# A graph network's second layer: edge directions computed chunk by chunk inside the loop, and eighteen buffers for the summed messages in place of eight

## The chip, the core and the metric

The kernel runs on one core of a Trainium2 chip. The core has a matrix engine (TensorE, PE in the profile; its weight loads are PEld), VectorE (DVE), ScalarE (ACT), GpSimd (POOL) and SyncE (SP). SP and POOL also issue DMAs here: SP plain loads and stores, POOL the indirect gathers and scatters. The metric is device time in microseconds, from launch to end; lower is better. A profiled execution gives for every instruction its start, its duration and what released it.

## The reference: what is computed

Two message-passing layers over a graph of 12500 nodes and 212500 edges (100000 pairs in both directions and 12500 loops, sorted by `dst`). A node has 160 features: 64 scalars and 32 vectors of three components. The change touches the second layer only. Cut to what matters there:

```python
h = relu(layernorm(x))
s, v = h[:, :64] @ W_nl0, einsum('nmi,mk->nki', h[:, 64:].reshape(N, 32, 3), W_nl1)
rhat = edge_attr / norm(edge_attr)                # (E, 3): the direction of an edge
w0..w4 = split(relu(edge_feature @ W_fc1) @ W_fc2)
xs, xv = s[dst], v[dst]
tp = concat(w0*xs, w3*(xv . rhat), (w1*xs) x sh1, w2*xv, w4*cross(xv, sh1)/sqrt2)   # sh1 = sqrt3 * rhat
agg = segment_sum(tp, src) / 32
```

For every edge the kernel thus needs its direction (three components over their length), the weights from its 64 edge features, and the row of its `dst` node; it forms 480 products per edge and adds them to the row of the `src` node.

## The kernel before

Edges are handled in tiles of 128 (one edge per partition): T = 1668 tiles. G = 4 tiles make a **quad** (417 of them, the passes `q` of the second layer's loop), CT = 12 tiles make a **chunk** (139, index `ch`), so a chunk is three quads. The work goes in stages: node maps, the first layer's loop over the edges, a short stage in between, the second layer's loop, and the output stage. All of the change lies in the second layer's loop and in the short stage right before it.

*Before the loop* (lines 684 to 692). A tile `r` of shape [128, 3, 1668] float32 (20016 bytes in every partition) is kept for the whole loop. Twelve passes each load 139 tiles' worth of edge vectors (`ea`, two buffers), and `directions` (line 613) makes the unit vectors: DVE squares (L615) and sums over the three components (L617), ACT takes the root (L618), DVE the reciprocal (L619) and the product (L620). These instructions are left to the scheduler's order.

*Loads of a chunk* (`sources`, `loads`, lines 699 to 715, all on SP): the `src` numbers of the chunk (`rows`, L702), the edge features (`ft`, L708), and four times the `dst` numbers of 384 edges (`to`, L713) and a window of 32 node rows (`fw`, L714). `picks` (L717) lets DVE compare `to` with the window's node numbers, which gives the 0/1 matrix `pick`.

*A quad in the loop* (lines 795 to 814) goes through these steps; the numbers tell for which quad a pass `q` does them:

- `hide(q + 4)`: PE multiplies the edge features (`hp`, L730), ACT takes the relu (`hs`, L732).
- `weights(q + 2, ...)`: PE makes the weights `wp` (L740; PSUM, two buffers).
- `picked(q + 3, ...)`: PE picks the `dst` rows (`gs`, L757) and ACT spreads them into `xs` and `xv` (L630 to L633).
- `turns(q + 2)`: ACT copies the quad's directions out of `r` (L624, L626) and the `src` numbers (L766) into spare columns of `wp`.
- `alike` (L665): DVE compares the quad's `src` numbers with each other (`same`); `second_messages` (L638): DVE makes the 480 products per edge (`msg`), eight instructions.
- `scattered(q, j)` for each of the four tiles: PE adds up equal `src` (`sm`, L771, two PSUM buffers), ACT copies the sum to `o` (L773, eight buffers), POOL issues the indirect DMA that adds `o` to the rows of accumulator `acc1[t % K]` in HBM (L775). K is 4, so tile t and tile t - 4 add to the same accumulator.

What sets the order: nearly every instruction in this loop goes through `keep`, which pins it on its engine behind everything that was traced on this engine before it. So PE, ACT and DVE run the loop in the order in which it is written:

```python
if (q + 4) % (CT // G) == 0:
    picks((q + 4) // (CT // G))
same = alike(...)
msg = second_messages(...)
scattered(q, 0, same, msg)
weights(q + 2, 0)
scattered(q, 1, same, msg)
picked(q + 3, 0)
weights(q + 2, 1)
scattered(q, 2, same, msg)
picked(q + 3, 1)
turns(q + 2)
scattered(q, 3, same, msg)
hide(q + 4)
```

Ahead of the loop stand `sources(0)`, `loads(0)`, `loads(1)`, `picks(0)`, `picks(1)` and the first `hide`, `weights`, `turns` and `picked`.

Of the kernel before, what the change touches and what calls it, by code (L numbers as in the profile page):

```python
# [9 lines left out]
F32 = mybir.dt.float32  # L10
# [3 lines left out]
AF = mybir.ActivationFunctionType  # L14
ALU = mybir.AluOpType
AX = mybir.AxisListType
# [3 lines left out]
P = 128  # L20
# [8 lines left out]
T = 1668  # L29
EP = T * P  # L30
PAD = N + 12
S = 3
# [8 lines left out]
G = 4  # L41
NQ1 = T // G
CT = 12
# [7 lines left out]
C1 = 480  # L51
# [5 lines left out]
def gnn_kernel(ctx: ExitStack, tc: tile.TileContext, a, out):  # L57
    nc = tc.nc
    tt = nc.vector.tensor_tensor
# [85 lines left out]
    for m in range(3):  # L145
        f0 = m * 96
        while f0 < (m + 1) * 96:
            k, p0 = divmod(f0, P)
            n = min((m + 1) * 96 - f0, P - p0)
# [127 lines left out]
    ep = edges0.enter_context(tc.tile_pool(name="ep0", bufs=1))  # L277
# [50 lines left out]
    def keep(i):  # L328
        tc.keep_in_program_order(i)
# [138 lines left out]
    with edges0 as st:  # L468
        ld = st.enter_context(tc.tile_pool(name="ld0", bufs=2))
        gp = st.enter_context(tc.tile_pool(name="gp0", bufs=6))  # L470
        wk = st.enter_context(tc.tile_pool(name="wk0", bufs=4))
# [49 lines left out]
        for gr in range(NG):  # L521
            hidden["now"] = gr
            q, a_ = divmod(gr, 2)
# [50 lines left out]
    with tc.tile_pool(name="okw", bufs=1) as wk, tc.tile_pool(name="okp", bufs=1, space=PSUM) as ps:  # L574
# [24 lines left out]
        m = NCB - 1  # L599
# [10 lines left out]
        nc.vector.tensor_copy(ok, over)  # L610


    def directions(su, r, ea, n):
        sq = su.tile([P, n, 3], F32, name="sq3")
        tt(sq, ea, ea, ALU.mult)  # L615
        no = su.tile([P, n], F32, name="no")
        nc.vector.tensor_reduce(no, sq, AX.X, ALU.add)  # L617
        nc.scalar.activation(no, no, AF.Sqrt)  # L618
        nc.vector.reciprocal(no, no)  # L619
        tt(r.rearrange("p m t -> p t m"), ea, no[:, :, None].to_broadcast([P, n, 3]), ALU.mult)  # L620

    def turned(r7, r, n, keep=lambda i: i):

        keep(nc.scalar.copy(r7[:, 0:6].rearrange("p (k m) t -> p k m t", m=3),  # L624
                            r[:, None, :, :].to_broadcast([P, 2, 3, n])))
        keep(nc.scalar.copy(r7[:, 6:7], r[:, 0:1]))  # L626
# [55 lines left out]


    with ExitStack() as st:
        ep = st.enter_context(tc.tile_pool(name="ep1", bufs=1))
        r = ep.tile([P, 3, T], F32, name="r")
        with tc.tile_pool(name="su1", bufs=2) as su:
            n = T // 12
            for i in range(12):
                ea = su.tile([P, n, 3], F32, name="ea")  # L690
                nc.sync.dma_start(ea, a["ea3"][:, i * n * 3:(i + 1) * n * 3])
                directions(su, r[:, :, i * n:(i + 1) * n], ea, n)
        ld = st.enter_context(tc.tile_pool(name="ld1", bufs=2))
        gp = st.enter_context(tc.tile_pool(name="gp1", bufs=3))
        wk = st.enter_context(tc.tile_pool(name="wk1", bufs=2))
        ps = st.enter_context(tc.tile_pool(name="ps1", bufs=1, space=PSUM))
        part = {}

        def sources(ch):
            if ch < NCH:  # L700
                part["rows", ch] = ld.tile([P, CE], I16, name="rows")
                nc.sync.dma_start(part["rows", ch], a["src_low"][:, ch * CE:(ch + 1) * CE].to_broadcast([P, CE]))  # L702

        def loads(ch):
            if ch >= NCH:
                return
            ft = ld.tile([P, CT // 2 * P], F32, name="ft")
            nc.sync.dma_start(ft, a["ea64"][:, ch * (CT // 2 * P):(ch + 1) * (CT // 2 * P)])  # L708
            to = ld.tile([P, S * P], I16, name="to")
            fw = ld.tile([P, D], F32, name="fw", bufs=3)  # L710
            for k in range(CW):
                e = ch * CE + k * S * P
                nc.sync.dma_start(to[k * W:(k + 1) * W, :], a["dst_low"][:, e:e + S * P].to_broadcast([W, S * P]))  # L713
                hidden["write"] = nc.sync.dma_start(fw[k * W:(k + 1) * W, :], ft1[bass.ds(row(ch * CW + k, NP - W), W), :])  # L714
            part["ft", ch], part["to", ch], part["fw", ch] = ft, to, fw

        def picks(ch):  # L717

            if ch < NCH:
                pick = ld.tile([P, S, P], F32, name="pick")  # L720
                keep(nc.vector.tensor_scalar(pick.rearrange("p t e -> p (t e)"), part["to", ch], nf[:, ch:ch + 1],
                                             None, op0=ALU.is_equal))
                part["pick", ch] = pick

        def hide(q):
            if q >= NQ1:
                return
            ch, k = divmod(q, CT // G)
            hp = ps.tile([P, 2 * P], F32, name="hp")
            keep(nc.tensor.matmul(hp, w1_1, part["ft", ch][:, k * 2 * P:(k + 1) * 2 * P], start=True, stop=True))  # L730
            part["hs", q] = wk.tile([P, 2 * P], F32, name="hs", bufs=3)
            keep(nc.scalar.activation(part["hs", q], hp, AF.Relu))  # L732

        def weights(q, c):
            if q >= NQ1:
                return
            if c == 0:
                part["wp", q] = ps.tile([P, G, 256], F32, name="wp", bufs=2)
            for h in range(2):
                keep(nc.tensor.matmul(part["wp", q][:, 2 * h + c, :224],  # L740
                                      part["hs", q][h * 64:(h + 1) * 64, c * P:(c + 1) * P],
                                      w1_2[h * 64:(h + 1) * 64], start=True, stop=True))

        def picked(q, i):
            if q >= NQ1:
                return
            ch, k = divmod(q, CT // G)
            if i == 0:
                part["xs", q] = gp.tile([P, G, S0], F32, name="xs")
                part["xv", q] = gp.tile([P, GV, G, V1], F32, name="xv")  # L750

            cut = S - k * G % S
            lo, hi = (cut, G) if i else (0, cut)
            gs = ps.tile([P, S, D], F32, name="gs")
            for j in range(lo, hi):
                u, v = divmod(k * G + j, S)
                keep(nc.tensor.matmul(gs[:, j - lo, :], part["pick", ch][u * W:(u + 1) * W, v, :],  # L757
                                      part["fw", ch][u * W:(u + 1) * W, :], start=True, stop=True))
            spread(part["xs", q][:, lo:hi], part["xv", q][:, :, lo:hi], gs[:, 0:hi - lo], keep)

        def turns(q):

            if q < NQ1:
                few = part["wp", q][:, 0, 224:256].rearrange("p (c t) -> p c t", t=G)
                turned(few[:, 0:7], r[:, :, q * G:(q + 1) * G], G, keep)
                keep(nc.scalar.copy(few[:, 7], idx["src"][:, q * G:(q + 1) * G]))  # L766
                part["few", q] = few

        def scattered(q, j, same, msg):
            sm = ps.tile([P, C1], F32, name="sm", bufs=2)  # L770
            keep(nc.tensor.matmul(sm, same[:, j, :], msg[:, j, S0:], start=True, stop=True))  # L771
            o = wk.tile([P, C1], F32, name="o", bufs=8)
            keep(nc.scalar.copy(o, sm))  # L773
            t = q * G + j
            nc.gpsimd.indirect_dma_start(  # L775
                out=acc1[t % K][:, :], out_offset=bass.IndirectOffsetOnAxis(ap=where[:, t:t + 1], axis=0),
                in_=o, in_offset=None, compute_op=ALU.add)

        sources(0)
        loads(0)
        loads(1)
        picks(0)
        picks(1)
        for q in range(4):
            hide(q)
        for q in range(3):
            if q < 2:
                weights(q, 0)  # L790
                weights(q, 1)
                turns(q)
            picked(q, 0)
            picked(q, 1)
        for q in range(NQ1):
            ch, k = divmod(q, CT // G)
            t0 = q * G
            if k == 0:
                sources(ch + 1)
                loads(ch + 2)  # L800
            if (q + 4) % (CT // G) == 0:
                picks((q + 4) // (CT // G))
            same = alike(wk, part["rows", ch][:, k * G * P:(k + 1) * G * P], part["few", q][:, 7], G, keep)
            msg = second_messages(wk, part["wp", q], part["xs", q], part["xv", q], part["few", q][:, 0:7], G, keep)
# [10 lines that stand above are left out]
# [14 lines left out]
    with tc.tile_pool(name="fwk", bufs=4) as wk, tc.tile_pool(name="fps", bufs=3, space=PSUM) as ps:  # L829
# [18 lines left out]
        for i in range(len(parts) + 1):  # L848
            now, ready = ready, added(i + 1)
            if now:  # L850
                t, s = now
# [3 lines left out]
            if gated:  # L855
                c, lo, n = parts[i - 1]
# [40 lines left out]
    with tc.If(flag > 0):  # L897
        with tc.tile_pool(name="gwk", bufs=1) as wk, tc.tile_pool(name="gps", bufs=1, space=PSUM) as ps:
# [14 lines left out]
            with tc.For_i(0, NQ) as q:  # L913
# [4 lines left out]
                for a_ in range(2):  # L918
# [4 lines left out]
                    for j in range(S):  # L923
                        t = HALF[a_][j]
# [43 lines left out]
            with tc.For_i(0, T // G) as q:  # L968
# [10 lines left out]
                for j in range(G):  # L979
                    h, c = divmod(j, 2)  # L980
# [67 lines left out]
```

## Time and profile before

| | |
|---|---|
| median of 13 runs | 6351.79 us (6329.0 to 6366.49) |
| profiled execution | 6369.05 us, span 6367.3 us, mean granted clock 0.916 |
| first layer's loop and before | up to 2564 us |
| twelve passes of directions | 2564.0 to 2606.4 us: DVE busy 34.6, ACT 3.8, PE 0 |
| second layer's loop, 2650 to 5940 us | of 3290 us: PE busy 3040, DVE 2457, ACT 1690, POOL 2603; granted clock 0.95 |
| first and last scatter (L775) | issued at 2635.7 and 5950.4 us |
| output stage, 5940 to 6367 us | of 427 us: PE busy 272, DVE 264, granted clock 0.50 |

How to read it: a time such as 4016.66 is counted from the start of the span. A line of the timeline has start, duration, engine, line of the kernel, operation, output<-inputs, and in square brackets how long the engine had been idle and what ended that. SPq, ACTq and POOLq are the engines' queues: waits and DMA issues, not busy time. A chunk is three quads, or twelve scatters, of the loop. A matmul in float32 stands in the records as two, and the ends of PE's records are modelled, so PE's starts say more than its busy time.

### The profile page before, as it was taken

How to read it: one execution, taken by the hardware profiler on the slowest of the kernel's cores; microseconds unless marked ns; L12 is line 12 of the kernel's file. 1: busy time of each engine (PE TensorE's matmuls, PEld its weight loads, DVE VectorE, ACT ScalarE, POOL GpSimd, SP SyncE). 2: the span in 40 equal slices, each digit the busy share in tenths (PEclk: the TensorE clock that was granted, in tenths of full speed). 3: DMA queues.
4: the chain of work that ended last, by engine and by line, in shares of the span. 5: the costliest groups of instructions: out<-in, count | busy, mean ns of one | idle time of the engine just before them, and what ended most of it. 6: DMA issues, size and time to landing. Idle time of an engine off the chain costs nothing.

```text
span 6367.3 us, 89060 instructions
## 1 busy us (share of the span) xinstructions
PE 5678.1 (89%) x22974; PEld 3189.1 (50%) x22974; DVE 4744.1 (75%) x12295; ACT 2582.1 (41%) x8173; POOL 4266.2 (67%) x3347
## 2 busy tenths in 40 slices
PE   6889999999999997699999999999999999999666
PEld 4555655566566664344444444444444444444465
DVE  5578888889888665677777777777777777777566
ACT  2223333333333332355555555555554554555211
POOL 0277777777777773377787777777777777777300
PEclk9999999999999998699999999999999999999655
DMA  9778888866555554599999999999999999999987
GB/s 347 248 237 258 262 249 257 246 162 164 158 162 154 132 131 112 103 167 162 165 168 162 166 165 162 167 164 167 166 167 162 165 168 163 165 168 163 231 286 255
DMA packets 704984, 1186.49 MB, mean 186 GB/s; under 512 B 119409, under 2 KB 554545, under 8 KB 704466
## 3 DMA queue, kind: packets, MB, share of 16 engines
q0 software_dynamic: 320256, 546.78, 54.7%
q1 hardware_dynamic: 370722, 617.39, 30.8%
q10 hardware_dynamic: 13488, 16.56, 0.7%
q8 instruction: 185, 3.03, 0.2%
q14 instruction: 333, 2.73, 0.1%
HBM read 528.25 MB, written 652.09 MB: 185 GB/s over the span
## 4 chain that ended last, share of the span: by engine, by line
PE 44%; DMA 37%; DVE 6%; issue 5%; POOL 4%; ACT 4%; SPq 0%; ACTq 0%; DVEq 0%; POOLq 0%
DMA acc<-o,where 28%; PE ag L497 11%; PE sm L771 8%; PE wp L323 5%; PE gs L757 3%; DMA sums<-so 3%; POOL acc L775 3%; PE hp L513 2%; PE wp L740 2%; DMA rows<-sums 2%; PE y L358 1%; ACT o L773 1%; DMA g<-ft,idx_src 1%; PE nd L255 1%; PE hp L730 1%
## 5 line engine op out<-in xcount | busy, mean ns | idle before, releaser
L775 POOL DMA_INDIRECT acc<-o,where x1668 | 2621.0, 1571 | 853.5 <-ACT o L773 270.9
L527 POOL DMA_INDIRECT g<-ft,idx_src x1668 | 1643.9, 986 | 817.1 <-issue 399.9
L771 PE MATMUL sm<-msg,same 128*128 128x480 f32 x3336 | 1850.3, 638 | 63.1 <-ACT o L773 58.3
L773 ACT COPY o<-sm 128x480 f32<-128x480 f32 x1668 | 930.0, 558 | 1502.1 <-DMA acc<-o,where 1013.8
L497 PE MATMUL ag<-pr,fac 128*128 128x320 f32 x3336 | 1086.2, 463 | 48.9 <-DVE pr L315 48.6
L757 PEld LDWEIGHTS gs<-fw,pick 32*128 32x128 f32 x3336 | 490.8, 191 | 791.4 <-ACT xv L633 422.3
L757 PE MATMUL gs<-fw,pick 32*128 32x160 f32 x3336 | 699.5, 330 | 189.7 <-ACT xv L633 188.4
L665 DVE TENSOR_TENSOR same<-rows,wp 128x512 f32<-128x512 int16 x417 | 286.8, 688 | 763.9 <-ACT wp L766 551.4
L771 PEld LDWEIGHTS sm<-msg,same 128*128 128x128 f32 x3336 | 547.1, 197 | 461.1 <-issue 224.5
L497 PEld LDWEIGHTS ag<-pr,fac 128*128 128x128 f32 x3336 | 606.6, 195 | 251.0 <-DVE pr L315 52.7
L500 ACT COPY so<-ag 128x161 f32<-128x161 f32 x556 | 163.3, 294 | 1007.2 <-PE ag L497 981.9
L638 DVE TENSOR_TENSOR pp<-xv,wp 128x1152 f32<-128x1152 f32 x417 | 561.6, 1347 | 0.0
L740 PE MATMUL wp<-w,hs 64*128 64x224 f32 x3336 | 556.8, 411 | 0.0
L550 DVE SCALAR_TENSOR_TENSOR seen<-rows,srcf,before 128x128 f32<-128x128 int16 x1668 | 528.8, 349 | 28.9 <-DMA rows<-in_src_low 28.7
L323 PE MATMUL wp<-w,hs 64*128 64x192 f32 x3336 | 524.2, 367 | 0.6 <-ACT hs L516 0.6
L740 PEld LDWEIGHTS wp<-w,hs 64*128 64x128 f32 x3336 | 259.6, 190 | 399.6 <-issue 399.5
L323 PEld LDWEIGHTS wp<-w,hs 64*128 64x128 f32 x3336 | 356.7, 191 | 170.5 <-issue 136.2
L534 DVE TENSOR_TENSOR fac<-hit,sh 128x384 f32<-128x384 bf16 x556 | 309.5, 557 | 157.1 <-PE ag L497 149.5
L315 DVE TENSOR_TENSOR pr<-wp,g 128x576 f32<-128x576 f32 x556 | 416.2, 749 | 0.0
L638 DVE TENSOR_TENSOR msg<-wp,xv 128x768 f32<-128x768 f32 x417 | 399.4, 958 | 14.3
L638 DVE TENSOR_TENSOR msg<-msg,wp 128x768 f32<-128x768 f32 x417 | 397.8, 954 | 14.5
L314 DVE TENSOR_TENSOR pr<-wp,g 128x384 f32<-128x384 f32 x556 | 307.5, 553 | 99.7 <-PE wp L323 55.6
(156 smaller groups left out, 6664.5 us busy)
## 6 DMA issues: line engine op xcount, KB each, us to landing
rows<-in_src_low SPq DMA_DIRECT2D x278, 384.0 KB
acc<-zero SPq DMA_DIRECT2D x132, 720.0 KB
sums<-acc SPq DMA_DIRECT2D x168, 480.0 KB
sums<-zero SPq DMA_DIRECT2D x2, 31878.0 KB
rows<-sums SPq DMA_DIRECT2D x84, 644.0 KB
ft<-in_ea SPq DMA_DIRECT2D x139, 384.0 KB
sums<-so SPq DMA_DIRECT2D x556, 80.5 KB
g<-ft,idx_src POOLq DMA_INDIRECT x1668
```

What stands on the lines that cost most here:

```text
L315: tt(o[:, :, :, S0:].rearrange("p t k (m u) -> p t k m u", m=3), w[:, :, :, None, S0:96].to_broadcast([P, n, 2, 3, V1]), split(g[:, :, S0: ...
L323: keep(nc.tensor.matmul(wp[:, j].rearrange("p (k u) -> p k u", k=2)[:, :, 0:96], hs[h * 64:(h + 1) * 64, c * P:(c + 1) * P], w0_2[h * 64:( ...
L497: keep(nc.tensor.matmul(ag[:, 0:2 * HB], fac[:, j].rearrange("p m w -> p (m w)"), pr[:, j, :], start=j == 0, stop=j == S - 1))
L527: nc.gpsimd.indirect_dma_start(out=g[:, j, :], out_offset=None, in_=ft0[:, :], in_offset=bass.IndirectOffsetOnAxis(ap=idx["src"][:, t0 + j ...
L534: tt(fac, hit[:, :, None, :].to_broadcast([P, S, 4, W]), hidden["sh", gr // CW][:, gr % CW * S:(gr % CW + 1) * S, :, None].to_broadcast([P ...
L550: nc.vector.scalar_tensor_tensor(seen, hidden["rows"][:, u * P:(u + 1) * P], srcf[:, t0 + j:t0 + j + 1], before, op0=ALU.is_equal, op1=ALU ...
L638: keep(tt(*args))
L740: keep(nc.tensor.matmul(part["wp", q][:, 2 * h + c, :224], part["hs", q][h * 64:(h + 1) * 64, c * P:(c + 1) * P], w1_2[h * 64:(h + 1) * 64 ...
L757: keep(nc.tensor.matmul(gs[:, j - lo, :], part["pick", ch][u * W:(u + 1) * W, v, :], part["fw", ch][u * W:(u + 1) * W, :], start=True, sto ...
L771: keep(nc.tensor.matmul(sm, same[:, j, :], msg[:, j, S0:], start=True, stop=True))
L773: keep(nc.scalar.copy(o, sm))
L775: nc.gpsimd.indirect_dma_start(out=acc1[t % K][:, :], out_offset=bass.IndirectOffsetOnAxis(ap=where[:, t:t + 1], axis=0), in_=o, in_offset ...
```

## The change

The tile `r` for all edges and the twelve passes before the loop go. `loads(ch)` also loads the edge vectors of its twelve tiles (`ea`, 128 rows of 144 bytes, two buffers), between `ft` and the first `to`. `picks(ch)` calls `directions` after the comparison, for twelve tiles, into `r` of [128, 3, 12] with three buffers, and with `keep`: all five instructions are pinned in the order of the program. `turns` reads the chunk's `r`. `o` gets eighteen buffers of 1920 bytes per partition (34560 in place of 15360 bytes).

```diff
-    def directions(su, r, ea, n):
+    def directions(su, r, ea, n, keep=lambda i: i):
         sq = su.tile([P, n, 3], F32, name="sq3")
-        tt(sq, ea, ea, ALU.mult)
+        keep(tt(sq, ea, ea, ALU.mult))
         no = su.tile([P, n], F32, name="no")
-        nc.vector.tensor_reduce(no, sq, AX.X, ALU.add)
-        nc.scalar.activation(no, no, AF.Sqrt)
-        nc.vector.reciprocal(no, no)
-        tt(r.rearrange("p m t -> p t m"), ea, no[:, :, None].to_broadcast([P, n, 3]), ALU.mult)
+        keep(nc.vector.tensor_reduce(no, sq, AX.X, ALU.add))
+        keep(nc.scalar.activation(no, no, AF.Sqrt))
+        keep(nc.vector.reciprocal(no, no))
+        keep(tt(r.rearrange("p m t -> p t m"), ea, no[:, :, None].to_broadcast([P, n, 3]), ALU.mult))
...
-        ep = st.enter_context(tc.tile_pool(name="ep1", bufs=1))
-        r = ep.tile([P, 3, T], F32, name="r")
-        with tc.tile_pool(name="su1", bufs=2) as su:
-            n = T // 12
-            for i in range(12):
-                ea = su.tile([P, n, 3], F32, name="ea")
-                nc.sync.dma_start(ea, a["ea3"][:, i * n * 3:(i + 1) * n * 3])
-                directions(su, r[:, :, i * n:(i + 1) * n], ea, n)
...
             nc.sync.dma_start(ft, a["ea64"][:, ch * (CT // 2 * P):(ch + 1) * (CT // 2 * P)])
+            ea = ld.tile([P, CT, 3], F32, name="ea")
+            nc.sync.dma_start(ea.rearrange("p t c -> p (t c)"), a["ea3"][:, ch * CT * 3:(ch + 1) * CT * 3])
+            part["ea", ch] = ea
...
                 part["pick", ch] = pick
+                part["r", ch] = ld.tile([P, 3, CT], F32, name="r", bufs=3)
+                directions(ld, part["r", ch], part["ea", ch], CT, keep)
...
-                turned(few[:, 0:7], r[:, :, q * G:(q + 1) * G], G, keep)
+                turned(few[:, 0:7], part["r", q // S][:, :, q % S * G:(q % S + 1) * G], G, keep)
...
-            o = wk.tile([P, C1], F32, name="o", bufs=8)
+            o = wk.tile([P, C1], F32, name="o", bufs=18)
```

## The prediction

> **What bounds the kernel now.** I read the waits inside the second layer's loop first (2650 to 5900 us of the span), then POOL's group there, the chain that ended last, and then one quad (four tiles, one pass of the loop) in order of time.
>
> The waits, longest in total (engine and line, what released it: us, times, longest):
>
> ```profile
> ACT o L773 <- DMA acc<-o,where: 993.3, 769, 4.4
> DVE same L665 <- ACT wp L766: 545.4, 273, 4.0
> ...
> POOL acc L775 <- ACT o L773: 265.1, 382, 2.2
> ```
>
> The first line makes the eighteen buffers look right: ACT stands 993 us waiting for a scatter to land and give a copied sum's buffer back. But is it ACT that holds the loop? POOL's group in the same stretch:
>
> ```profile
> L775 POOL DMA_INDIRECT acc<-o,where x1636 | 2571.1, 1572 | 680.9 <-ACT o L773 265.1 <-issue 194.8 <-DMA acc<-o,where 131.6
> ```
>
> 3250 us for 1636 scatters is 1.987 us a scatter, 23.84 us for a chunk of twelve. An issue takes 1.55 us, and the timeline never shows less than 0.30 us between two: 1.86 us, 22.3 us a chunk. So POOL is within 7% of its own floor: of its 680.9 us of idle time 1636 x 0.30 = 491 is that floor, and 190 us is real. What ends those 190? The chain, from 4061 us on:
>
> ```profile
> 4061.27 5.31 DMA acc<-o,where
> 4066.58 0.02 issue
> 4066.61 0.02 POOLq L775
> 4066.62 0.22 issue
> 4066.85 7.29 DMA acc<-o,where
> ```
>
> A scatter lands and releases POOL's queue (not ACT): the issues between are at 4063.13 and 4064.99, after 4061.27, so at 4066.85 it is the landing of a tile a few places earlier. Tiles four apart add into the same accumulator (t % 4) and have to follow each other. Buffers for o do not shorten that. Taking POOL's starts one by one, 234 begin more than 0.35 us after the issue before them, 180 us in all, and in every one the landing of tile t-4 came after ACT's copy of tile t. When POOL starts tile t, ACT has usually finished four or five more. **So POOL, tied to the landings four back, sets the loop, and ACT's 993 us is waiting room.**
>
> PE is the runner-up. One quad, DVE's and PE's lines that matter:
>
> ```profile
> 4016.66 0.69 DVE L665 TENSOR_TENSOR same<-rows,wp 128x512 f32<-128x512 int16 x1 [2.82 <-ACT wp L766]
> ...
> 4021.69 0.96 DVE L638 TENSOR_TENSOR msg<-wp,xv 128x768 f32<-128x768 f32 x1
> ...
> 4022.98 0.60 PE L730 MATMUL hp<-ft,w 128*128 128x256 f32 x2
> ...
> 4023.41 0.97 PE L771 MATMUL sm<-msg,same 128*128 128x480 f32 x2
> 4023.64 0.39 ACT L732 ACTIVATE hs<-hp 128x256 f32<-128x256 f32 x1
> ```
>
> Here is the point of the case. DVE starts `same` of quad q at 4016.66, as soon as the turn of q is copied (two iterations before, in turns(q)), and ends its last product at 4022.65; PE's first sum of q starts at 4023.41, 0.77 us later. Over the loop that slack has a median of 1.19 us, is under 0.77 in a quarter of the quads, and 0.15 us, PE's bare wait for DVE, in one of twenty: PE is fed just in time, and only because DVE works **one quad ahead** (same(q) starts 8.8 us before the relu of hide(q+3) ends, 6.6 at the least). The same PE pair stood at 4016.54 one quad before, so PE runs a quad in 6.87 us when nothing stops it, 20.6 us a chunk against POOL's 23.84: 3.2 us of lead per chunk.
>
> **Part 1, the twelve early directions go.** SP issued their first load at 2564.02 and the loop's first load at 2606.45:
>
> ```profile
> 2606.45 0.33 SPq L702 DMA_DIRECT2D rows<-in_src_low  x1
> ...
> 2620.94 0.42 DVE L721 TENSOR_SCALAR pick<-to,nf 128x384 f32<-128x384 int16 x1 [6.83 <-DMA to<-in_dst_low]
> ```
>
> So the loop's loads move up by 42.4 us. Given back: chunk 1's root is pinned on ACT ahead of the first relu, and it follows pick(1) on DVE, which waits for chunk 1's last window load. Before, the first relu (2612.86) came 6.41 us after the first load, and pick(1) 14.49. After: 14.49 + 2 issues of ea on SP (0.42 each, as L708) + pick 0.42 + square, sum and root 0.8 = 16.5, so relu is 10.1 us later. From relu to the first scatter everything is PE's chain, which moves with it. Net **-32 us**.
>
> **Part 2, directions in the loop.** The trace has these forms at 139 tiles alone, so each cost lies between rows: square (36 elements) 0.19 (128x32, L429) to 0.59 (L615), I take 0.2; sum 0.15 (L605, 13 elements) to 0.57 (L617), 0.25; root 0.20 (L223) to 0.32 (L618), 0.2; reciprocal 0.16 (L225) to 1.02 (L619), by its length 0.23; product 0.19 (L429) to 0.90 (L620), 0.2: nearest to the small rows each time, as twelve tiles are. Together 1.1 us (0.9 to 3.4), 139 times: about 150 us on engines with room (DVE 149 us busy of 200, ACT 103). No table load: ACT's roots (12) and relus (417) follow each other now without one. As work, nothing.
>
> **The order is what costs.** keep pins each instruction behind all that was traced on its engine. picks(ch) comes before iteration Q = 3ch-4. So the root stands on ACT behind the last relu of iteration Q-1, that of hide(Q+3), and on DVE reciprocal and product stand before same(Q). DVE can no longer start same(Q) an iteration ahead: it waits for a relu which PE releases only *after its last sum of Q-1*. And behind same(Q) and the products PE waits with its first sum of Q. In the times above: relu ends 4024.03, root 4024.25, reciprocal and product 4024.75, same to last product 5.98 (4016.66 to 4022.65), PE 0.15 later: 4030.9 instead of 4023.4. **PE stands 7.4 us, once per chunk** (7.2 by the least rows; 9.7 if all five cost what 139 tiles do). The quads after it are fed in time: 5.98 of DVE under 6.87 of PE.
>
> **And then it restarts at half clock.** The granted clock after a stop (times; busy us of PE, PEld, DVE, ACT, POOL; PEclk, DMA share, GB/s):
>
> ```profile
> 4004.40:4007.80 3.40, 3.40 (x7) 2.11 (x8) 0.00 (x0) 1.51 (x8) 2.02 (x2) 0.50 1.13 207
> 4007.80:4011.30 3.50, 3.50 (x9) 1.41 (x8) 3.40 (x4) 1.46 (x4) 2.89 (x3) 0.51 0.97 151
> 4011.30:4014.70 3.40, 3.40 (x13) 1.54 (x14) 2.40 (x6) 1.34 (x5) 2.79 (x3) 1.00 1.08 202
> ```
>
> A stop of 1.64 us ended at 4004.35; from there to 4011.07 PE did gs x4, sm, hp, sm, wp, which the chain shows at full clock as 0.74 + 1.00 + 0.43 + 0.81 + 0.58 = 3.56 us: 3.2 us lost. A stop of 7.4 us is longer than any there is now in the loop (3.5), so I price each restart near this row: 3.0 us (0 to 3.4 where the half clock lasts 6.8 us).
>
> The Trainium skill, "TensorE: Matmul & The Clock Gate", section "What's actually happening", says that for modelling the ramp is under 1% of a kernel's span and should not be fitted. By that the restarts would cost at most some 64 us; by the row, 137 x 3.0 = 411. The rule has one ramp in mind; here there would be one per chunk, so the row decides.
>
> Chunk after: 20.6 + 7.4 + 3.0 = 31.0 us, above POOL's 23.84: PE's chain becomes the bound, and the landings are late no more. 137 chunks are picked inside the loop (0 and 1 before it): 137 x (31.0 - 23.84) = **+981 us**.
>
> **Part 3, eighteen buffers.** They let ACT copy 18 ahead of the landings instead of 8. With POOL as the bound that moves waiting room; with PE as the bound o is always free. 0, but for the end: POOL's last issue (5950.4) trails ACT's last copy (5941.3) by 9 us, and would by 2: -7. The skill's "Perfetto Trace Analysis", section "Optimization Strategy", says that a repeating gap can mean too few buffers for the next tile; by that I would take off up to the 190 us of POOL's excess. The chain shows another releaser, so I take off none.
>
> ea's loads: 18 KB, 139 times, 2% of the 8.2 MB that SP's queue moves in 200 us; 0 here, at most 10 us if POOL stayed the bound. SP has room (it waits 852 us at L708 alone).
>
> **Sum.** -32 + 981 - 7 = +942, on the profiled execution (6369 us; span 6367.3) 7311; on the median of 13 runs (6352, 17 lower) **7294, say 7290 us**.
>
> **Rivals.**
> 1. The stop without the half clock: chunk 28.0, 137 x 4.16 = 570 - 39: 6883. For it: the granted clock is still 0.95 over the loop, with 53 stops of over 1.5 us in it. Against: the rows above. 10%.
> 2. The half clock lasts as at the loop's start, where PE is dense from 2631 on and gets its clock only at 2649: 18 us, 9 us lost per chunk, 37 us: +1802 - 39: 8115. Against: that start came out of a stage at 0.50 throughout; in the loop the row above is the usual case. 4%.
> 3. Faster. The buffers hide the stop: PE's lead is 3.2 us a chunk, and eighteen sums hold 14 x 1.86 = 26 us of POOL's work. Where stop and restart stay under 3.2 us, POOL never sees them and the 32 us at the start remain, less up to 10 for ea: 6330; with POOL's excess gone too, 6140. It decides from 3.2 us on, and I count 10.4. For it: ACT is four tiles ahead now. 4%.
> 4. The directions are not ordered as I read it (the scheduler lets the root through early), and the loop's extra wait eats just the 32 us: 6352. 2%.
>
> The forecast has 80%. **Range 6850 to 7460**: from rival 1 with a 7.2 us stop (137 x 3.95 - 39) to a stop of 7.6 with 4.0 lost; the five operations at the price of 139 tiles (7610) are left out, since their rows have twelve times the elements. Faster by over 0.2% (about what a measurement of this kernel can tell from no change) 0.04, within 0.02, slower 0.94.
>
> **What the profile would show.** DVE idle before L619 or behind it, released by ACT's L618, about 137 times 7 us or more of lost lead; PE idle before L771, released by DVE, some 7 us, 137 times; half clock after each; the chain made of PE, DVE and ACT instead of landings; ACT's wait for landings at L773 near nothing; POOL's first scatter near 2603 instead of 2635.7. I am wrong if L771's stops are short, or if POOL's issues still come every 1.99 us.

## The result, and the profile after

After the change the kernel takes 7438.2 us (median of 8 runs, 7425.2 to 7451.8), before it 6349.7 (37 runs, 6329.0 to 6366.5): a ratio of 1.171, interval 1.170 to 1.173. The forecast was 7290 us, 148 us less than measured, and the range, 6850 to 7460, holds the time. The profiled execution after took 7447.8 us, span 7446.0, mean granted clock 0.835; the span is 1078.7 us longer than before.

In the kernel after, three lines fewer stand ahead of the loop's code: the loop's sum is L768 (was L771), its copy L770 (L773), its scatter L772 (L775), the relu L729 (L732). Directions are still L615 to L620. The granted clock over the span, first before, then after (40 slices each):

```profile
PEclk9999999999999998699999999999999999999655
```

```profile
PEclk9999999999999677788888777888777788778755
```

The second layer, which ran at 0.9 and more, now runs at 0.7 to 0.8. The waits inside the loop after (2650 to 7000 us; total us, times, longest):

```profile
ACT o L770 <- PE sm L768: 2342.0, 1187, 8.5
POOL acc L772 <- ACT o L770: 1467.4, 693, 7.3
...
DVE no L619 <- ACT no L618: 1137.0, 136, 9.8
PE sm L768 <- DVE msg L638: 972.3, 136, 7.4
```

Read it from below. DVE waits 136 times for the root; PE waits 136 times for DVE's last product, 7.1 us each; ACT waits for PE, POOL for ACT. The 993 us in which ACT waited for landings are gone from the list. POOL's group in the same stretch, where the landings come no more as a releaser of weight:

```profile
L772 POOL DMA_INDIRECT acc<-o,where x1640 | 2551.0, 1555 | 1799.4 <-ACT o L770 1467.4 <-issue 129.7 <-ACT hs L729 63.2
```

One stop, in the timeline after (start, duration, engine, line, operation; in brackets how long idle before and what ended it):

```profile
4033.64 0.59 PE L727 MATMUL hp<-ft,w 128*128 128x256 f32 x2
...
4034.36 0.39 ACT L729 ACTIVATE hs<-hp 128x256 f32<-128x256 f32 x1
4034.63 0.21 ACT L618 ACTIVATE no<-no 128x12 f32<-128x12 f32 x1
4034.88 0.23 DVE L619 RECIPROCAL no<-no 128x12 f32<-128x12 f32 x1 [9.59 <-ACT no L618]
4035.14 0.22 DVE L620 TENSOR_TENSOR r<-ea,no 128x36 f32<-128x36 f32 x1
4035.25 0.68 DVE L665 TENSOR_TENSOR same<-rows,wp 128x512 f32<-128x512 int16 x1
...
4040.27 0.96 DVE L638 TENSOR_TENSOR msg<-wp,xv 128x768 f32<-128x768 f32 x1
...
4041.38 1.94 PE L768 MATMUL sm<-msg,same 128*128 128x480 f32 x2 [7.14 <-DVE msg L638]
```

PE's `hp` ends, ACT's relu follows, behind it the root, behind that DVE's reciprocal, product, `same` and all eight products, and only then does PE go on. The five operations are short, 0.21 to 0.23 us in the three rows here; the 9.59 us in brackets are DVE standing idle ahead of the reciprocal, with the next quad's comparison and products pinned behind it. And PE's first sum after the stop takes 1.94 us where it takes 1.07 at full clock. The windows from that restart on (us, then busy us of PE, PEld, DVE, ACT, POOL; granted clock, DMA share, GB/s):

```profile
4041.00:4044.40 3.40, 3.02 (x7) 1.11 (x7) 3.37 (x5) 0.56 (x1) 0.21 (x1) 0.50 0.21 40
4044.40:4047.80 3.40, 3.40 (x10) 1.29 (x10) 2.58 (x6) 0.94 (x4) 2.32 (x2) 0.84 0.48 55
4047.80:4051.20 3.40, 3.40 (x15) 1.92 (x14) 0.80 (x2) 2.59 (x9) 2.20 (x3) 1.00 0.87 102
```

Where the 1078.7 us are: the first layer's last store came 8.6 us later (2572.1 instead of 2563.5, in code that did not change); from there to the first scatter 40.1 us instead of 72.2, so -32.1; from the first scatter to the last 4415.9 instead of 3314.7, so +1101.2; the output stage +1. The forecast for the sum of these was 942.

### The profile page after: what moved, and what is told of

Same layout as the page of the kernel before. It is cut to its first block, busy times and chain, and to the rows that moved or that the text cites. A ratio compares the mean times of both kernels' runs of the same rounds, so it can differ in the third digit from the quotient of the medians.

```text
span 7446.0 us, 89664 instructions
## 1 busy us (share of the span) xinstructions
PE 6057.9 (81%) x22974; PEld 3322.5 (45%) x22974; DVE 4786.0 (64%) x12803; ACT 2630.3 (35%) x8300; POOL 4239.9 (57%) x3347
## 4 chain that ended last, share of the span: by engine, by line
## 5 line engine op out<-in xcount | busy, mean ns | idle before, releaser
L772 POOL DMA_INDIRECT acc<-o,where x1668 | 2594.5, 1555 | 1949.7 <-ACT o L770 1485.4
L768 PE MATMUL sm<-msg,same 128*128 128x480 f32 x3336 | 2110.7, 720 | 983.5 <-DVE msg L638 983.5
L770 ACT COPY o<-sm 128x480 f32<-128x480 f32 x1668 | 929.7, 557 | 2394.6 <-PE sm L768 2373.9
L768 PEld LDWEIGHTS sm<-msg,same 128*128 128x128 f32 x3336 | 608.6, 220 | 1424.6 <-issue 1254.7
L754 PEld LDWEIGHTS gs<-fw,pick 32*128 32x128 f32 x3336 | 518.3, 201 | 702.8 <-issue 601.7
L619 DVE RECIPROCAL no<-no 128x12 f32<-128x12 f32 x139 | 31.7, 228 | 1157.1 <-ACT no L618 1157.1
L754 PE MATMUL gs<-fw,pick 32*128 32x160 f32 x3336 | 735.5, 343 | 3.0 <-ACT xv L633 3.0
L737 PE MATMUL wp<-w,hs 64*128 64x224 f32 x3336 | 645.1, 470 | 0.0
L737 PEld LDWEIGHTS wp<-w,hs 64*128 64x128 f32 x3336 | 300.0, 220 | 500.7 <-issue 500.5
L323 PEld LDWEIGHTS wp<-w,hs 64*128 64x128 f32 x3336 | 359.0, 192 | 172.2 <-issue 141.1
```

The source lines that it names most:

```text
L323: keep(nc.tensor.matmul(wp[:, j].rearrange("p (k u) -> p k u", k=2)[:, :, 0:96], hs[h * 64:(h + 1) * 64, c * P:(c + 1) * P], w0_2[h * 64:( ...
L737: keep(nc.tensor.matmul(part["wp", q][:, 2 * h + c, :224], part["hs", q][h * 64:(h + 1) * 64, c * P:(c + 1) * P], w1_2[h * 64:(h + 1) * 64 ...
L772: nc.gpsimd.indirect_dma_start(out=acc1[t % K][:, :], out_offset=bass.IndirectOffsetOnAxis(ap=where[:, t:t + 1], axis=0), in_=o, in_offset ...
```

## The experiments

The theory: the root, pinned behind the relu, stops PE once per chunk; PE then restarts at half clock; buffers and the work itself cost nothing. The rivals: the cost is the loads or the five operations themselves; the buffers matter; the half clock is only shown beside the stop and costs little by itself. The runs came from three chips. On two of them the kernel before takes 7060 and 7009 us, 655 and 706 us more than on the first. The profiles of the changed kernels show that time in the first layer, while the second layer's loop is the same to 0.1 us in the kernel that was profiled on two chips (early18 and early18b). So times are compared as ratios on one chip, and between chips by the loop: from the first scatter's issue to the last, in the profiled execution.

**1. The root moved ahead, with the square and the sum that feed it (early18).** Square, sum and root of a chunk are written two quads before its `picks`, behind the second scatter of a quad; reciprocal and product stay where the change has them, and everything is still pinned.

```diff
-                directions(ld, part["r", ch], part["ea", ch], CT, keep)
+                if ch < 2:
+                    roots(ch)        # square, sum, root
+                units(ch)            # reciprocal, product
...
             scattered(q, 1, same, msg)
+            if k == 0:
+                roots(ch + 2)
```

> The changed kernel, same work, same loads, eighteen buffers; only the square, the sum and the root of chunk ch are written two quads earlier (behind the second scatter of quad 3ch-6), reciprocal and product stay where they were. My theory: the stop of 7.1 us per chunk comes from the place of the root alone, so it goes, the half clock with it, and POOL's chain of landings sets the loop again: 6350 less 32 at the start plus 0 to 10 for the loads, 6315 to 6335 us. Rival A, the work or the loads in the loop cost the time: above 7000. Rival B, the eighteen buffers also take away POOL's waits: 6140 to 6250.

Measured: 6324.4 us (6311.4 to 6340.6), ratio 0.9949 (0.9932 to 0.9966). Loop 3298.6 us, against 4415.9 in the kernel after. Its timeline at one root:

```profile
4010.34 0.19 DVE L729 TENSOR_REDUCE no<-sq 128x12 f32<-128x36 f32 x1
...
4015.45 0.22 ACT L730 ACTIVATE no<-no 128x12 f32<-128x12 f32 x1
...
4018.28 0.22 DVE L736 RECIPROCAL no<-no 128x12 f32<-128x12 f32 x1
4018.53 0.22 DVE L737 TENSOR_TENSOR r<-ea,no 128x36 f32<-128x36 f32 x1
4018.65 0.68 DVE L665 TENSOR_TENSOR same<-rows,wp 128x512 f32<-128x512 int16 x1
4019.81 0.39 ACT L746 ACTIVATE hs<-hp 128x256 f32<-128x256 f32 x1
```

The root ends 2.6 us before the reciprocal starts, which has no bracket: DVE waits for nothing there, and `same` starts before the relu, as in the kernel before. Same loads, same five operations, same buffers: 1114 us less than the kernel after. **The whole loss is the place of these three instructions**, and of the three it is the root that DVE waited for in the kernel after (136 times, 1137.0 us). In the loop the waits and POOL's group are those of before again:

```profile
ACT o L787 <- DMA acc<-o,where: 1019.3, 821, 4.0
```

```profile
L789 POOL DMA_INDIRECT acc<-o,where x1646 | 2587.5, 1572 | 664.7 <-ACT o L787 237.3 <-issue 199.7 <-DMA acc<-o,where 123.0
```

ACT waits 1019 us for landings, with eighteen buffers as it waited 993 with eight.

**2. Eight buffers, with the stop and without it (o8, early8).** Each is a kernel above with one number back:

```diff
-            o = wk.tile([P, C1], F32, name="o", bufs=18)
+            o = wk.tile([P, C1], F32, name="o", bufs=8)
```

> The changed kernel with eight buffers for the summed messages in place of eighteen; the directions stay in the loop. My theory: PE's chain of stops sets the loop, so a buffer is always free in time, and the time stays at 7438 us within 15 (7420 to 7455). Rival, the eighteen buffers matter (they give time back, or their place costs some): it moves by more than 30 us either way.

> The kernel with the early root, but eight buffers for the summed messages. My theory: POOL waits for the landing of tile t-4, not for a copied sum, so eight are as good as eighteen: within 15 us of the one with eighteen, 6315 to 6340. Rival B (the buffers take away POOL's waits): 100 to 190 us slower than with eighteen.

Measured: o8, made from the kernel after, 7437.2 us (7425.7 to 7451.7), ratio 1.1705 (1.1682 to 1.1727), where the kernel after has 1.1713. early8 6325.3 us (6315.4 to 6329.9), ratio 0.9949 (0.9935 to 0.9962), where early18 has 0.9949. With eighteen, ACT ran up to 15 tiles ahead of POOL, with eight up to 5; of POOL's starts that were late, 221 and 230, each came after the landing of the tile four back, none after ACT. So the ten buffers move where sums wait and nothing that the time shows, whichever engine is the bound.

**3. The stop without the half clock (fill).** PE gets work in the stop: behind the relu ahead of each stop the product `hp` is made fifteen times more, into its own buffer, and not used.

```diff
             keep(nc.scalar.activation(part["hs", q], hp, AF.Relu))
+            if q >= 4 and q % (CT // G) == 2:
+                for _ in range(15):
+                    keep(nc.tensor.matmul(hp, w1_1, part["ft", ch][:, k * 2 * P:(k + 1) * 2 * P], start=True, stop=True))
```

> The changed kernel with fifteen repeats of the last edge-feature product (same inputs, same output tile, written again with the same values) behind the relu ahead of each stop, which keep PE busy while it would wait; the order and its wait stay. My theory: the stop stays at 7.1 to 7.5 us, but the clock stays up, so the 3.8 us per chunk that I put down to the half clock go: 137 x 3.8 = 520 less, 6890 to 6960 us, granted clock in the loop above 0.97. Rival, the half clock has another cause than PE's stop: no faster than 7400.

Measured: 6904.8 us (6902.1 to 6909.3), ratio 1.0863 (1.0846 to 1.0880). The wait for the root is still there in the waits, and the clock over 2700 to 6400 us is full:

```profile
DVE no L619 <- ACT no L618: 1047.5, 135, 8.0
```

```profile
2700.00:6400.00 3700.00, 3624.38 (x14298) 2077.06 (x14299) 2423.80 (x4234) 1658.52 (x5700) 2475.87 (x1591) 1.00 0.95 142
```

A chunk takes 27.94 us: three quads of 6.87 and a stop of 7.31, within 0.02. More work on PE, and 533 us faster than the kernel after: 533 / 137 = 3.9 us per chunk is what the half clock costs, taken by itself. The rival by which it costs little falls. (The repeats only fill PE's time: the quad with the stop takes 14.18 us in both kernels.)

**4. Is POOL really tied to the landings four back (acc8)?** early18 with eight accumulators in rotation in place of four (`t % (2 * K)`), so that the landing that a scatter has to follow is that of the tile eight back. Only four of them are cleared and added up at the end, so half of the sums are left out.

> The early root with eight accumulators in place of four for the scatters (tile t waits for the landing of tile t-8); only the first four are cleared and added up at the end, so half of the sums is left out, and the stages before and after do the same work. My theory: POOL's waits for the landing four back are what is left over its floor of 1.86 us per scatter; they are 160 to 180 us in the loop and go: 6324 less 130 to 180, 6145 to 6195 us, POOL's excess idle time in the loop under 30 us. Rival (the DMA engines are full anyway, or PE takes over at its 6.87 us per quad plus half-clock stretches): less than 60 us gained.

Measured: loop 3120.8 us, against 3298.5 with four on the same chip (start, below): 178 less. (Ratio to the kernel before 0.969, 0.967 to 0.972.) POOL's group in the loop (3350 to 6350 us of its span):

```profile
L789 POOL DMA_INDIRECT acc<-o,where x1604 | 2512.8, 1567 | 489.1 <-issue 206.7 <-DMA acc<-o,where 102.8 <-ACT o L787 75.3
```

1604 gaps of 0.30 are 481 of the 489 us: POOL is at its floor, with 2 late starts in the whole loop in place of 221. The step that read POOL's 190 us of excess as the landings of tile t-4, and not as ACT or buffers, holds.

**5. The directions not pinned (loose).** The kernel after, with `keep` left out of one call:

```diff
-                directions(ld, part["r", ch], part["ea", ch], CT, keep)
+                directions(ld, part["r", ch], part["ea", ch], CT)
```

> The changed kernel with the five instructions of directions left to the scheduler's order instead of being pinned (one word less: no keep in the call). The comparison, the products and the copies stay pinned behind what was traced before them. My theory: the scheduler lets the root through as soon as the sum is there, ahead of the relu that ACT waits for, and the stop goes: 6315 to 6345 us. Rival: the root is put where it was, since the copies behind it are pinned to it: 7400 to 7450.

Measured: ratio 0.9942 (0.9923 to 0.9961), loop 3300.4 us. The scheduler puts the root ahead by itself (at one chunk, at 4612.24 us, ahead of the relu at 4615.01), and the stop is gone. So it is the pinning at this place that makes the loss, not the loads or work in the loop.

**6. The start shortened (start).** early18, with chunk 1's square, sum and root moved into the first quad and its reciprocal and product into the second, so that the first relu does not wait for them.

```diff
-                if ch < 2:
+                if ch == 0:
                     roots(ch)
-                units(ch)
+                if ch != 1:
+                    units(ch)
...
+            if q == 1:
+                units(1)
             scattered(q, 0, same, msg)
...
+            if q == 0:
+                roots(1)
```

> The kernel with the early root, and besides chunk 1's square, sum, root, reciprocal and product moved from ahead of the loop into its first two quads, so that the first relu on ACT no longer follows pick(1). My theory: the 10 us that I counted as given back at the start come back: 6324 less 10, 6305 to 6322 us, first scatter about 30 us after the first layer's last store instead of 40. Rival: the start is set by the window loads (14.5 us until the last has landed) whatever ACT does: same as the early root, 6324.

Measured: from the first layer's last store to the first scatter 32.4 us, where early18's own form takes 39.8: 7.4 of the 10 us expected. In the time it can't be told from early18: ratio 0.9959 (0.9943 to 0.9975), and early18 had just that on the third chip (early18b, below). So most of the 10 us that the prediction gave back at the start do come from this wait; as a gain in the whole time they are too small to show here.

**7. The root one quad ahead instead of two (mid, and again as midb beside early18b).**

```diff
+            if k == 1:
+                roots(ch + 2)
             same = alike(...)
...
             scattered(q, 1, same, msg)
-            if k == 0:
-                roots(ch + 2)
```

> The early root, but square, sum and root written only one quad before the reciprocal, ahead of the comparison of quad Q-1, so on ACT behind the relu that ends quad Q-2. My theory: reciprocal then waits until some 0.9 us after PE's first sum of Q-1, the products of Q end 7.3 us after it, and PE, which comes back after 6.9, stands 0.5 us per chunk and under POOL's slack of 3 us: 6320 to 6345 us. Rival (any wait of DVE for ACT at that place costs the full stop): above 7000.

> The kernel with the early root (two quads ahead, eighteen buffers) once more, beside the one with the root one quad ahead. My theory (both only remove the stop): the two agree within 15 us, 0.995 of the kernel before. Rival (the root one quad ahead gives something of its own, as its loop of 3262 us against 3299 says): it is 30 us or more faster.

> The root one quad ahead, again, beside the one two quads ahead. My theory, stop removed and nothing else: 0.995 of the kernel before, within 15 us of the early root. Rival (short stops of PE, 0.4 us and more in every chunk, spread its work, so that scatters land sooner): 30 us or more faster than the early root, loop of 3260 us again, fewer half-clock stretches (22 against 57).

Measured: mid 0.9910 (0.9884 to 0.9936), loop 3261.5 us; side by side on the third chip, early18b 6979.1 us, 0.9959 (0.9943 to 0.9975), loop 3298.5, and midb 6945.5 us, 0.9901 (0.9881 to 0.9921), loop 3261.1. That the stop stays away with one quad's room was expected. That mid is faster than early18 was not: my expectation that the place, once early enough, has no effect of its own fell in both repetitions, by 34 to 37 us. In midb's loop POOL's excess is 154 us (181 in early18b), its issues of over 1.6 us are 82 (132), and PE's half-clock stretches 22 (50). The excess accounts for 27 of the 37 us, and shorter issues (2608.5 us in all, against 2619.3) for the rest. What makes both shorter, and whether the clock leads or follows, stays open.

**8. The pieces together (midstart, midstart8).** mid with start's edit, with eighteen and with eight buffers.

> Root one quad ahead and chunk 1's directions inside the first quads, eighteen buffers. Both gains add if they are separate: 7 us less than the root one quad ahead alone; first scatter some 32 us after the first layer's last store instead of 40.

> The same with eight buffers. My theory (POOL never waits for a copied sum): within 15 us of the one with eighteen. Rival (with PE's small stops the longer queue of copied sums starts to matter): 20 us or more slower than with eighteen.

Measured: midstart 6933.6 us, ratio 0.9892 (0.9872 to 0.9912), first scatter 32.4 us after the first layer's last store; midstart8 6929.8 us, 0.9887 (0.9867 to 0.9907). Their ratios are the lowest of all that compute the whole result, 1.1% under the kernel before, though midb's interval reaches over both; the 7 us of the start can't be told apart in the time. The eight buffers are enough. Eighteen buffers with `r` kept for all edges, the third combination, was not tried.

## Why the prediction was right

By its steps, in its own order:

- **What bounds the loop before: POOL, tied to the landings four back.** Held. acc8 takes the tie away and the loop comes down by 178 us, to POOL's floor; more buffers alone (early18 against early8) give nothing.
- **Start, -32 us.** -32.1 measured. The first relu came 16.75 us after the loop's first load; 16.5 was worked out. The scatter itself came at 2612.2 and not near 2603, because the stage before ended 8.6 us later in that execution.
- **The five operations.** 0.19, 0.19, 0.21, 0.23 and 0.22 us: 1.04 together for the 1.1 taken, no table load at 139 changes between root and relu, and no cost as work (early18).
- **The stop, 7.4 us per chunk.** The quad with the stop takes 14.18 us instead of 6.87: 7.31. (The times that the sum was read from give 7.47, 4030.88 less 4023.41; it took 7.4.)
- **PE becomes the bound.** A chunk takes 20.6 + 7.31 + half clock; POOL waits for ACT, ACT for PE, and ACT's wait for landings is gone. With the stop taken away (early18, loose) POOL binds again.
- **The half clock, 3.0 us per chunk: the term that was too small.** It measured 3.9, from both sides: a chunk takes 31.83 us, less 20.62, less 7.31, is 3.90; and fill gets 3.9 back. The sum was 127 us too low from the first to the last scatter: 137 x 0.9 = 123 for the half clock and 7 for the tail (below), less 137 x 0.09 = 12 for the shorter stop; some 9 us stay open. The 3.0 was read from one restart after a short stop, where full clock came after 6.7 us and 3.2 us were lost. No restart of the usual pattern was like it. In two chunks of three full clock came 4.1 or 4.9 us after the restart, with chunks of 29.95 and 30.29 us, 2.0 and 2.4 us lost. In the third the half clock held for 15.6 us and the chunk took 35.33, 7.4 us lost. That one price for all came as near to their mean of 3.9 as it did was in part luck. Rival 2 took a return of 18 us for all chunks; one nearly as long came for one in three.
- **Eighteen buffers, 0.** Held twice (experiment 2). The Trainium skill's "Perfetto Trace Analysis", section "Optimization Strategy", says that a gap that repeats on the engine that should be saturated can mean too few buffers for the next tile. Here POOL sets the loop, and its gaps were not of that kind: with ten buffers more its late starts are 221 in place of 230. ACT's 993 us, on an engine with room, is not the gap that the page speaks of.
- **The tail, -7.** Did not come. POOL's last issue trails the end of ACT's last copy by 8.1 us, as by 8.6 before. The last three quads have no stop in them; from the first sum of the fourth-last quad to that of the last PE takes 19.03 us, less than the 22.3 that POOL needs for twelve scatters, so POOL is behind again at the end; I had carried the loop's state to its last pass.

Rival 3, buffers that hide the stop, named the right point of decision: 3.2 us a chunk, against 11.2 measured. Rivals 1 and 4 fall with fill and with the timeline.

On the clock, the runs say more than the one row of the prediction: by fill the restarts cost 533 of 7438 us, 7.2% of the kernel. The Trainium skill ("TensorE: Matmul & The Clock Gate", section "What's actually happening") puts the penalty of the ramp under 1% of a typical kernel's span; taken for this kernel, whose stop repeats in a loop, it would be far too low.

## What to carry to other kernels

An instruction that is pinned in the order of the program ties two engines at its place: before putting one into a loop, see what stands ahead of it on its own engine, who waits behind the instruction that it feeds, and give it a quad of room; that decided 1114 us here, and the work itself nothing that these runs can tell. A long wait for a buffer need not be a lack of buffers: ask what releases the engine that sets the loop (here POOL, by landings), and whether the waiting one is ahead of it anyway. A repeated stop of PE cost its length (7.31 us) and a restart at half clock (3.9 us in the mean) here, and the restart was not one number (2.0, 2.4 or 7.4 us lost): take its range from several restarts.

## What the runs showed of the hardware that was not expected

- The return to full clock after a like stop of 7.1 us took 4.1, 4.9 or 15.6 us from the restart, in a pattern that repeats over three chunks. The half-clock stretches in the records from 2650 us on are 6.8 us (46 of them), 10.2 (44) and 20.5 us (46): two, three and six times 3.41 us. In this trace the clock changes only at points of a fixed grid of 3.413 us (none is more than 0.011 us off it), and three chunks, 29.95 + 30.29 + 35.33 = 95.57 us, are 28 steps of the grid. So the three kinds come in turn because every third restart falls on the same place in a step. After the restart 0.7, 1.5 or 1.9 us of the step are left; with 0.7 and 1.5 the clock is full after one more step, with 1.9 after four more, though PE is busy throughout them, as at the restart at 4579.48 us. The last step at half clock and the first at full clock there:

```profile
4591.64:4595.06 3.42, 3.42 (x9) 1.52 (x7) 2.98 (x4) 1.50 (x3) 1.57 (x1) 0.50 0.58 79
4595.06:4598.47 3.41, 3.41 (x17) 1.73 (x14) 3.27 (x8) 1.40 (x4) 2.85 (x2) 1.00 0.80 102
```

Why the restart that comes earliest in its step has the longest return was not tried.
- Fifteen products that nobody uses made the kernel 533 us faster than the kernel after, by keeping PE's clock full.
- A root one quad ahead gives a loop 37 us shorter than a root two quads ahead, though both take the stop away. The cause is open.
- On two other chips the first layer took some 660 to 700 us longer, with the second layer's loop of the same kernel at 3298.5 and 3298.6 us. In the first layer (200 to 2500 us) POOL then waits 646 us for DVE in place of 295, and the granted clock is 0.85 in place of 0.96; the cause was not tried.
